# Graph attention on one core: for half the heads, the exponentials of two blocks are added by GpSimd and multiplied with 1e-8 once

## The chip, the cores and the metric

The kernel runs on one core of one Trainium2 chip. The metric is the time of one execution in device microseconds; the figure for a kernel is the median of several runs.

## The reference

Sixteen graphs (b) of 1024 nodes with 128 features go through two layers. Cut to what matters:

```python
# layer 0: attention with 8 heads of 16 features, over the edges of adj
h = relu(layernorm(x))
q, k, v = heads(h @ Wq.T + bq), heads(h @ Wk.T + bk), heads(h @ Wv.T + bv)
scores = where(adj == 0, -inf, einsum('bhnd,bhmd->bhnm', q, k) / sqrt(16))
attn = softmax(scores, axis=-1) * adj
attn = attn / (attn.sum(axis=-1, keepdims=True) + 1e-08)
x = x + merge(einsum('bhnm,bhmd->bhnd', attn, v)) @ Wo.T + bo
# layer 1: edges are "dilated" (row by row, every second neighbour of a long row is
# removed, which changes the rows after it), then three graph convolutions with batch norm
x = x + sage(relu(layernorm(x)), dilate(adj), ...)
```

With e = exp(score), masked, and w = e * adj, the attention of one node n is sum over m of w * v, divided by sum of w + 1e-8 * sum of e. The change is about the last term, 1e-8 times the sum of e.

## The kernel before

The program has two stages. In the first, attention of layer 0 runs together with the dilation of the edges (which needs only adj); in the second, the three graph convolutions run. Attention is TensorE, ScalarE and VectorE work; dilation is mostly VectorE work. A function takes a step of the one (`attention`), then steps of the other (`dilation`) up to a budget, so that both share the engines. The order of the instructions on TensorE (PE), ScalarE (ACT) and VectorE (DVE) is the order in which the program writes them; each engine works its queue in order. GpSimd (POOL) and the load queue on SyncE (SP) are in order too.

Attention goes over 16 graphs b, two halves c of the nodes n (512 each), eight blocks m of 128 neighbours, and two groups g of four heads: 512 half-steps. One half-step (b, c, m, g) does this:

- `scores` (L521 on): PE writes the mask and the scores of four heads into two PSUM tiles q = 0, 1 of 128x1024 (`sc`, L536 and L542). When a count of dilation comes first, the scores of the next half-step are drawn ahead of it (`made["next"]`).
- `values` (L466 on) of the half-step before: PE multiplies w with v, which has a column of ones for the sum of w (L469), and then e with `eps8`, a matrix that is 1e-8 in that same column (L474). Both add to one PSUM tile `acc[g]` from m = 0 to m = 7. This is the eps product of the text: four matmuls, which are eight in the trace.
- ACT makes e out of the scores, two tiles of 128x1024 (L579; ring of four tiles "e").
- DVE makes w = e * aT, two tiles (L584; ring of four tiles "w"), where aT is the transposed block of adj.

For g = 0 the block of adj that will be needed two steps later is transposed (`turn_over`, L487 on; `load` has brought it three steps ahead into a ring of three tiles "a"), and its mask is copied to other partitions by SP's queue (L498, L499).

Beside this, `conclude` divides the finished `acc` of the last half graph: `rd` is the reciprocal of the denominator (L395), and GpSimd copies it into `rden` (L399). At the end `judge` (L945 on) tests on DVE, over all of `rden`, that the denominators were in a sane range (L952, L953); if a test fails, a slow version of everything runs. `layer_norm_relu` uses GpSimd once for each norm, for a power of 8 numbers per partition (L272), whose result DVE takes up a half-step later (L274).

Of the kernel before, what the change touches and what calls it, by code (L numbers as in the profile page):

```python
# [10 lines left out]
F32 = mybir.dt.float32  # L11
BF = mybir.dt.bfloat16
# [4 lines left out]
ALU = mybir.AluOpType  # L17
AX = mybir.AxisListType
# [3 lines left out]
P = 128  # L22
# [2 lines left out]
NORM_EPS = 1e-12  # L25
BIG = 1e30
ROUNDS = 7


def tri(k):  # L30
# [4 lines left out]
def swept(ctx: ExitStack, tc: tile.TileContext, t: dict, out: bass.AP, flag: bass.AP):  # L35
# [8 lines left out]
    nc = tc.nc  # L44
    x, adj, nodemask = t["x"], t["adj"], t["nodemask"]
    B, N, D = x.shape
    H = 8
    HD = D // H
    NB = N // P
    HB = NB // 2  # L50
    HN = N // 2
# [112 lines left out]
    def first_part(p1):  # L164
# [15 lines left out]
        def load(i, queue=nc.sync):  # L180
            if i >= len(turns):
                return
            b, c, m = turns[i]
            a = pool.tile([P, HB, P], F32, name=f"a_{b}_{c}_{m}", tag="a", bufs=3)
            queue.dma_start(
                a, adj[b, c * HN : (c + 1) * HN, m * P : (m + 1) * P].rearrange("(k p) m -> p k m", p=P)
            )
            tiles[i] = a
# [36 lines left out]
            yield  # L225

        def node_masks():
            nr_f = pool.tile([B * NB, P], F32, name="nr_f", tag="w", bufs=4)
            nc.vector.tensor_copy(nr_f, nr_i)
            mps = ps_d.tile([P, 512], F32, name="mps", tag="d")  # L230
            nc.tensor.transpose(mps[:, : B * NB], nr_f, ident[: B * NB, : B * NB])
            nc.vector.tensor_copy(mf, mps[:, : B * NB])
            nc.vector.tensor_tensor(mf2, mf, mf, ALU.mult)
            nc.vector.tensor_scalar(
                kill.rearrange("p b k -> p (b k)"), mf, 0.0, -1e5, ALU.is_equal, ALU.mult
            )
# [16 lines left out]
        nc.vector.memset(eps8, 0.0)  # L253
        nc.vector.memset(eps8[:, HD : HD + 1], 1e-8)

        rden = one.tile([P, B * 2, HB, H], BF, name="rden")

        def layer_norm_relu(dst, src, name, lo=0, hi=NB):

# [117 lines left out]
        def conclude(b, c, acc, xt):  # L377

            yield False
            cx = small.tile([P, HB, H, HD], F32, name=f"cx_{b}_{c}", tag="cx", bufs=1)  # L380
            oTs = []
            for g in range(2):
                oT = small.tile([P, HN], F32, name=f"oT_{b}_{c}_{g}", tag="oT", bufs=2)
                nc.scalar.copy(oT, acc[g])
                oTs.append(oT)
            for g in range(2):
                yield True
                on = ps_m.tile([P, HB, 4, 32], F32, name=f"on_{b}_{c}_{g}", tag="m")
                for i in range(HB):
                    nc.tensor.transpose(  # L390
                        on[:, i, :, :].rearrange("p h d -> p (h d)"), oTs[g][:, i * P : (i + 1) * P], ident
                    )
                yield "evict by VectorE"
                rd = small.tile([P, HB, 4], F32, name=f"rd_{b}_{c}_{g}", tag="rd", bufs=2)
                nc.vector.reciprocal(rd.unsqueeze(3), on[:, :, :, HD : HD + 1])  # L395
                nc.vector.tensor_tensor(
                    cx[:, :, g::2, :], on[:, :, :, :HD], rd.unsqueeze(3).to_broadcast([P, HB, 4, HD]), ALU.mult
                )
                nc.gpsimd.tensor_copy(rden[:, 2 * b + c, :, 4 * g : 4 * g + 4], rd)  # L399
            yield True  # L400
            pc = ps_m.tile([P, 512], F32, name=f"pc_{b}_{c}", tag="m")
            for i in range(HB):
                nc.tensor.transpose(
                    pc[:, i * P : (i + 1) * P], cx[:, i, :, :].rearrange("p h d -> p (h d)"), ident
                )
            yield "evict"
            cxT = small.tile([P, HN], F32, name=f"cxT_{b}_{c}", tag="oT", bufs=2)
            nc.scalar.copy(cxT, pc)
            yield True
            pr = ps_m.tile([P, HB, D], F32, name=f"pr_{b}_{c}", tag="m")  # L410
            start_with(pr, bias3[:, 1, :])
            for i in range(HB):
                nc.tensor.matmul(
                    pr[:, i, :], cxT[:, i * P : (i + 1) * P], wts["Wo"], start=False, stop=(i == HB - 1)
                )
            yield "evict by VectorE"
            part = xt[:, c * HB : (c + 1) * HB, :]
            nc.vector.tensor_tensor(part, part, pr, ALU.add)
            if c == 1:
                yield False  # L420
                nc.sync.dma_start(x1_d[b], xt)
                yield from layer_norm_relu(xt, xt, f"b{b}")
                nc.sync.dma_start(h0_d[b], xt)
# [38 lines left out]
        def attention():  # L462

            late = None

            def values(acc, v1, m, g, es, ws):  # L466

                for j in range(4):
                    nc.tensor.matmul(  # L469
                        acc[g][32 * j : 32 * j + 32, :], v1[:, m, 2 * j + g, :],  # L470
                        ws[j // 2][:, j % 2, :], start=(m == 0), stop=False,
                    )
                for j in range(4):
                    nc.tensor.matmul(  # L474
                        acc[g][32 * j : 32 * j + 32, :], eps8,
                        es[j // 2][:, j % 2, :], start=False, stop=(m == NB - 1),
                    )

            def turn_over(i):
# [69 lines left out]
            for i, (b, c, m) in enumerate(turns):  # L549
                if m == 0:  # L550
                    if c == 0:
                        xt, _, _, v1 = ready[b]
                    acc = [ps_o.tile([P, HN], F32, name=f"acc_{b}_{c}_{g}", tag=f"acc{g}") for g in range(2)]
                    if c == 0 and b + 1 < B:
                        take_on(prepare(b + 1), len(beside))
                    if c == 1 and b + 1 == B:
                        take_on(begin_sage(), len(beside))
                if c == 1 and m == HB + 1:
                    load_x(b + 2)
                load(i + 3)  # L560
                aT = tiles[i][0]
                for g in range(2):
                    scs = scores(i, g)
                    go_on_with(f"half {c}")
                    if g == 0:
                        go_on_with("first")
                        turning = turn_over(i + 2)
                        next(turning, None)
                    else:
                        go_on_with(True)  # L570
                    if late:
                        values(*late)
                    elif g == 0:
                        node_masks()
                        go_on_with(True)
                    es, ws = [], []
                    for q in range(2):
                        e = pool.tile([P, 2, HN], F32, name=f"e_{b}_{c}_{m}_{g}_{q}", tag="e", bufs=4)
                        nc.scalar.activation(e, scs[q], AF.Exp, scale=1.0 / math.sqrt(HD))  # L579
                        es.append(e)  # L580
                    go_on_with("evict by VectorE")
                    for q in range(2):
                        w = pool.tile([P, 2, HN], F32, name=f"w_{b}_{c}_{m}_{g}_{q}", tag="w", bufs=4)
                        nc.vector.tensor_tensor(w, es[q], aT.to_broadcast([P, 2, HN]), ALU.mult)  # L584
                        ws.append(w)
                    late = (acc, v1, m, g, es, ws)
                    if m == 0 and g == 0 and i > 0:

                        take_on(conclude(*done), 1 if c == 0 else 0)
                        go_on_with(False)  # L590
                    go_on_with("evict")
                    if g == 0:
                        next(turning, None)
                    go_on_with(False)
                    if i + g + 1 < len(turns):
                        made["next"] = partial(scores, i + g, 1 - g)
                    yield
                tiles.pop(i)
                done = (b, c, acc, xt)
# [345 lines left out]
        def judge():  # L945
# [1 line left out]

            still = small.tile([P, 3], F32, name="still", bufs=1)
            nc.vector.tensor_reduce(still[:, 0:1], changed, AX.X, ALU.add)
            rd = rden.rearrange("p a i h -> p (a i h)")  # L950
            fits = pool.tile([P, B * NB * H], F32, name="fits", tag="kT")
            nc.vector.tensor_scalar(fits, rd, 1e25, None, ALU.is_le)  # L952
            nc.vector.scalar_tensor_tensor(  # L953
                fits, rd, 1e-30, fits, ALU.is_ge, ALU.mult, accum_out=still[:, 1:2]
            )
            nc.vector.tensor_scalar(still[:, 1:2], still[:, 1:2], -1.0, float(B * NB * H), ALU.mult, ALU.add)
            nc.vector.tensor_tensor(still[:, 0:1], still[:, 0:1], still[:, 1:2], ALU.add)
            nc.vector.tensor_reduce(still[:, 1:2], signs, AX.XYZ, ALU.add)
# [224 lines left out]
    with tc.manual_schedule(  # L1183
# [6 lines left out]
        for L in range(3):  # L1190
# [8 lines left out]
            for b in range(B):  # L1199
# [4 lines left out]
                for c in range(2):  # L1204
                    i = (L * B + b) * 2 + c
# [689 lines left out]
```

## Time and profile before

| what | us |
| --- | --- |
| median of 3 runs | 3561.78 (3560.0 to 3562.39) |
| the profiled execution, its own time | 3556.3 |
| span of the profiled execution | 3554.4 |
| busy in the span: PE / DVE / ACT / POOL | 3445.8 / 3174.0 / 2290.9 / 179.0 |

The profile is one execution. A group line gives line of code, engine, operation, tile written <- tiles read, the shape and the count; then busy us in all, the mean ns of one, and the time that the engine stood idle before such instructions with what ended it. A line in order of time gives start, length, engine, line, operation. A view by stage gives for each stretch the busy us of each engine. L numbers are lines of the kernel before. A wait is put down to the event that came last.

### The profile page before, as it was taken

The page shows a single profiled execution, that of the slowest core. Times are in us where ns is not written, and L with a number is a line of the kernel's source. Part 1 is how long each engine was busy: PE and PEld are TensorE (multiplying, and loading weights), DVE is VectorE, ACT ScalarE, POOL GpSimd, SP SyncE. Part 2 cuts the span into 40 slices and gives each one's busy share as a digit, 9 for nine tenths or more (in the row PEclk, how much of TensorE's full clock was granted, in tenths as well). Part 3 has the DMA queues.
Part 4 walks back from the last instruction along what each step waited for, and adds up shares of the span by engine and source line. Part 5 has one row for each costly group of instructions (what it writes and reads, how often), then busy time and mean ns, then how long its engine had stood idle before and what let it go on. Part 6 is the DMA issues. An engine that isn't in the chain of part 4 may idle for free.

```text
span 3554.4 us, 86070 instructions
## 1 busy us (share of the span) xinstructions
PE 3445.8 (97%) x34855; PEld 1893.8 (53%) x34855; DVE 3174.0 (89%) x5254; ACT 2290.9 (64%) x3781; POOL 179.0 (5%) x253
## 2 busy tenths in 40 slices
PE   8999999999999999999999999999999899999997
PEld 3333333333333333333333333338999899989996
DVE  7999999999989999999999999987878788878886
ACT  6699689679769869968976885873232333322224
POOL 2000000000000000000000000000000000000000
PEclk9999999999999999999999999999999999999999
DMA  7356356447537636735754763667999799989995
GB/s 231 102 169 201 123 159 199 142 135 214 168 111 222 195 116 201 227 111 170 235 157 133 235 205 110 209 213 285 331 331 326 266 328 328 329 295 333 333 332 184
DMA packets 650122, 772.27 MB, mean 217 GB/s; under 512 B 173264, under 2 KB 569168, under 8 KB 637424
## 3 DMA queue, kind: packets, MB, share of 16 engines
q1 hardware_dynamic: 632672, 708.58, 61.7%
q0 software_dynamic: 15456, 57.30, 4.9%
q8 instruction: 275, 4.51, 0.5%
q14 instruction: 135, 1.11, 0.1%
q10 hardware_dynamic: 1584, 0.79, 0.1%
HBM read 508.50 MB, written 157.29 MB: 187 GB/s over the span
## 4 chain that ended last, share of the span: by engine, by line
PE 48%; DVE 39%; ACT 6%; DMA 3%; issue 3%; SPq 1%; POOL 0%; ACTq 0%; DVEq 0%; POOLq 0%
DVE w L584 16%; PE pg L1108 16%; PE sc L542 6%; PE acc L469 5%; PE acc L474 5%; DVE wr L872 4%; PE pn L1079 2%; DVE hit L807 2%; ACT e L579 2%; PE sc L536 2%; PE own L1094 2%; PE py L1023 2%; DMA nomask<-nomask 1%; PE pt L1145 1%; DVE aT L142 1%
## 5 line engine op out<-in xcount | busy, mean ns | idle before, releaser
L584 DVE TENSOR_TENSOR w<-e,aT 128x1024 f32<-128x1024 f32 x1024 | 1204.2, 1217 | 91.2 <-ACT e L579 90.9
L579 ACT ACTIVATE e<-sc 128x1024 f32<-128x1024 f32 x1024 | 990.9, 1020 | 376.1 <-PE sc L542 375.0
L1108 PE MATMUL pg<-y,aT 128*128 128x128 f32 (+1 forms) x6144 | 738.0, 275 | 0.0
L1108 PEld LDWEIGHTS pg<-y,aT 128*128 128x128 f32 x6144 | 712.4, 192 | 0.0
L469 PE MATMUL acc<-w,v_both 128*32 128x512 f32 x4096 | 673.1, 607 | 8.6 <-DVE w L584 3.8
L474 PE MATMUL acc<-e,eps 128*32 128x512 f32 x4096 | 650.5, 596 | 0.0
L542 PE MATMUL sc<-qT,kT 32*128 32x512 f32 x4096 | 584.8, 641 | 0.0
L142 DVE SCALAR_TENSOR_TENSOR aT<-mr,aT 128x1024 f32<-128x1024 bf16 x384 | 458.9, 1217 | 0.0
L474 PEld LDWEIGHTS acc<-e,eps 128*32 128x32 f32 x4096 | 165.9, 110 | 295.1 <-issue 285.2
L1131 ACT ACTIVATE sq<-o 128x512 f32<-128x512 f32 x96 | 60.5, 631 | 363.4 <-DVE o L1126 363.4
L872 DVE TENSOR_TENSOR_SCAN wr<-rk 128x1024 f16<-128x1024 bf16 x128 | 291.7, 2279 | 0.0
L536 PEld LDWEIGHTS <-never 32*32 32x32 bf16 x8192 | 79.1, 88 | 345.3 <-issue 323.6
L536 PE MATMUL sc<-nomask,never 32*32 32x512 bf16 x8192 | 249.6, 385 | 12.5 <-ACT e L579 8.0
L469 PEld LDWEIGHTS acc<-w,v_both 128*32 128x32 f32 x4096 | 106.4, 108 | 233.9 <-DVE w L584 140.2
L542 PEld LDWEIGHTS sc<-qT,kT 32*128 32x128 f32 x4096 | 160.1, 183 | 116.6 <-issue 116.6
L487 PEld LDWEIGHTS pa<-ident,a 128*128 128x128 f32 x1024 | 108.2, 142 | 182.4 <-issue 143.5
L1146 ACT COPY hT<-pt 128x512 f32<-128x512 f32 x96 | 56.3, 587 | 224.2 <-PE pt L1145 223.2
L1126 DVE SCALAR_TENSOR_TENSOR o<-pg,rdeg,mine 128x128 f32<-128x128 f32 x384 | 108.1, 344 | 92.2 <-PE pg L1108 90.4
L885 ACT ACTIVATE wr<-wr,th 128x1024 f16<-128x1024 f16 x128 | 148.0, 1156 | 46.7 <-DVE wr L872 45.8
L487 PE MATMUL pa<-ident,a 128*128 128x128 f32 x1024 | 168.7, 288 | 7.0 <-DMA a<-in_adj 6.3
L494 ACT ACTIVATE nomask<-aT 128x512 bf16<-128x512 f32 x256 | 161.4, 630 | 8.1
L490 ACT COPY aT<-pa 128x512 f32<-128x512 f32 x256 | 151.6, 592 | 11.5 <-PE pa L487 6.8
(222 smaller groups left out, 3949.8 us busy)
## 6 DMA issues: line engine op xcount, KB each, us to landing
aT<-aT_d SPq DMA_DIRECT2D x94, 2048.0 KB, 9.0
mr<-mr_d SPq DMA_DIRECT2D x188, 512.0 KB, 5.8
aT_d<-aT SPq DMA_DIRECT2D x256, 256.0 KB, 4.0
a<-in_adj SPq DMA_DIRECT2D x253, 256.0 KB, 4.0
ad<-in_adj SPq DMA_DIRECT2D x112, 512.0 KB, 4.1
nomask<-nomask SPq DMA_DIRECT2D x512, 96.0 KB, 2.7
nomask<-nomask SPq DMA_DIRECT2D x512, 64.0 KB, 2.6
nomask<-nomask SPq DMA_DIRECT2D x512, 32.0 KB, 2.6
```

What stands on the lines that cost most here:

```text
L142: nc.vector.scalar_tensor_tensor(part, mrs[h][:, j : j + 2, :].rearrange("p j n -> p (j n)"), 0.0, part, ALU.is_equal, ALU.mult)
L469: nc.tensor.matmul(acc[g][32 * j : 32 * j + 32, :], v1[:, m, 2 * j + g, :], ws[j // 2][:, j % 2, :], start=(m == 0), stop=False,)
L474: nc.tensor.matmul(acc[g][32 * j : 32 * j + 32, :], eps8, es[j // 2][:, j % 2, :], start=False, stop=(m == NB - 1),)
L487: nc.tensor.transpose(pa[:, k * P : (k + 1) * P], a[:, k, :], ident)
L490: nc.scalar.copy(aT[:, 0, :], pa)
L494: nc.scalar.activation(nomask[:, 0, :], aT[:, 0, :], AF.Relu, bias=1.0, scale=-1e38, accum_out=zeros[:, i : i + 1])
L536: nc.tensor.matmul(scs[j // 2][to : to + 32, j % 2, :], never[rows, rows], nomask[rows, j, :], start=True, stop=False, tile_position=(32 * ...
L542: nc.tensor.matmul(scs[j // 2][:, j % 2, :], kT[rows, mm], qTs[c][rows, g, :], start=False, stop=True, tile_position=(32 * j, 0),)
L579: nc.scalar.activation(e, scs[q], AF.Exp, scale=1.0 / math.sqrt(HD))
L584: nc.vector.tensor_tensor(w, es[q], aT.to_broadcast([P, 2, HN]), ALU.mult)
L872: nc.vector.tensor_tensor_scan(wrs[b], rk(b, 1, N + 1), rk(b, 2, N + 2), -1023.0, ALU.add, ALU.add)
L1108: nc.tensor.matmul(pg[:, i // 2, at : at + width], aT[:, j, i * P : (i + 1) * P], y[:, j, :width], start=(j == 0), stop=(j == NB - 1),)
```

## The change

For the heads of g = 0 and the blocks m = 0 to 5, the e of an even block is kept (two tiles "kept"); GpSimd adds the e of the odd block to it, and the eps product is made once for both blocks, at the head of the next even half-step of g = 0. For g = 1 and for m = 6 and 7 nothing changes. To have room for the kept tiles, the ring w has three tiles for four, the ring a two for three (the third first tile borrows one that dilation uses later), and `rden` goes: GpSimd tests `rd` at once, in four small instructions, and adds up the results, which `judge` sums.

```diff
+PAIRED = 6
...
-            a = pool.tile([P, HB, P], F32, name=f"a_{b}_{c}_{m}", tag="a", bufs=3)
+            where, tag = (shared, "ad") if i == 2 else (pool, "a")
+            a = where.tile([P, HB, P], F32, name=f"a_{b}_{c}_{m}", tag=tag, bufs=2)
...
-        rden = one.tile([P, B * 2, HB, H], BF, name="rden")
+        rfits = one.tile([P, HB, 4], F32, name="rfits")
+        nc.gpsimd.memset(rfits, 0.0)
...
-                nc.gpsimd.tensor_copy(rden[:, 2 * b + c, :, 4 * g : 4 * g + 4], rd)
+                fit = small.tile([P, 2, HB, 4], F32, name=f"fit_{b}_{c}_{g}", tag="fit", bufs=1)
+                nc.gpsimd.tensor_scalar(fit[:, 0], rd, 1e25, None, ALU.is_le)
+                nc.gpsimd.tensor_scalar(fit[:, 1], rd, 1e-30, None, ALU.is_ge)
+                nc.gpsimd.tensor_tensor(fit[:, 0], fit[:, 0], fit[:, 1], ALU.mult)
+                nc.gpsimd.tensor_tensor(rfits, rfits, fit[:, 0], ALU.add)
...
             def values(acc, v1, m, g, es, ws):
 
                 for j in range(4):
                     nc.tensor.matmul(
                         acc[g][32 * j : 32 * j + 32, :], v1[:, m, 2 * j + g, :],
                         ws[j // 2][:, j % 2, :], start=(m == 0), stop=False,
                     )
+                if g == 1 or m >= PAIRED:
+                    exponentials(acc, g, es, m == NB - 1)
+
+            def exponentials(acc, g, es, stop):
                 for j in range(4):
                     nc.tensor.matmul(
                         acc[g][32 * j : 32 * j + 32, :], eps8,
-                        es[j // 2][:, j % 2, :], start=False, stop=(m == NB - 1),
+                        es[j // 2][:, j % 2, :], start=False, stop=stop,
                     )
...
                 for g in range(2):
+                    if both and g == 0 and m % 2 == 0:
+                        exponentials(*both, False)
+                        both = None
                     scs = scores(i, g)
...
-                        e = pool.tile([P, 2, HN], F32, name=f"e_{b}_{c}_{m}_{g}_{q}", tag="e", bufs=4)
+                        kept = g == 0 and m < PAIRED and m % 2 == 0
+                        e = pool.tile(
+                            [P, 2, HN], F32, name=f"e_{b}_{c}_{m}_{g}_{q}",
+                            tag="kept" if kept else "e", bufs=2 if kept else 4,
+                        )
...
-                        w = pool.tile([P, 2, HN], F32, name=f"w_{b}_{c}_{m}_{g}_{q}", tag="w", bufs=4)
+                        w = pool.tile([P, 2, HN], F32, name=f"w_{b}_{c}_{m}_{g}_{q}", tag="w", bufs=3)
...
                     late = (acc, v1, m, g, es, ws)
+                    if g == 0 and m < PAIRED and m % 2 == 0:
+                        first = es
+                    elif g == 0 and m < PAIRED:
+                        for to, e in zip(first, es):
+                            nc.gpsimd.tensor_tensor(to, to, e, ALU.add)
+                        both = (acc, g, first)
...
-            rd = rden.rearrange("p a i h -> p (a i h)")
-            fits = pool.tile([P, B * NB * H], F32, name="fits", tag="kT")
-            nc.vector.tensor_scalar(fits, rd, 1e25, None, ALU.is_le)
-            nc.vector.scalar_tensor_tensor(
-                fits, rd, 1e-30, fits, ALU.is_ge, ALU.mult, accum_out=still[:, 1:2]
-            )
+            nc.vector.tensor_reduce(still[:, 1:2], rfits, AX.XY, ALU.add)
```

More of the change, by code (lines that the diff above doesn't have):

```diff
@@ L227, in node_masks @@
         def node_masks():
-            nr_f = pool.tile([B * NB, P], F32, name="nr_f", tag="w", bufs=4)
+            nr_f = pool.tile([B * NB, P], F32, name="nr_f", tag="w", bufs=3)
             nc.vector.tensor_copy(nr_f, nr_i)
@@ L464, in attention @@
             late = None
+            first = both = None
             def values(acc, v1, m, g, es, ws):
```

## The prediction

> **What bounds the kernel now.** I read the busy shares first, then the same by stage, then the groups of the attention stage, then single places in order of time.
>
> ```profile
> 0.00:2412.00 2412.00, 2362.34 (x25784) 860.84 (x25784) 2264.10 (x3414) 1917.83 (x3003) 135.75 (x173) 1.00 0.58 173
> 2412.00:3554.40 1142.40, 1083.49 (x9071) 1032.99 (x9071) 909.90 (x1842) 373.03 (x779) 43.23 (x80) 0.98 0.87 311
> ```
>
> These two rows are the stages (window, length, busy of PE, PEld, DVE, ACT, POOL, then the granted clock, DMA share, GB/s). The change lies in the first, up to the last products of attention at 2412 us. There VectorE (DVE) is busy for 2264.1 of 2412 us, so 147.9 us are all the idle time it has. TensorE (PE) reads 98%, but a matmul that waits for an operand counts as busy there, so its true load is lower. GpSimd (POOL) is nearly free: 135.75 us. The clock is at full speed, so it is no term of the sum. The second stage (1142.4 us) is left as it is.
>
> ```profile
> L584 DVE TENSOR_TENSOR w<-e,aT 128x1024 f32<-128x1024 f32 x1024 | 1204.2, 1217 | 91.2 <-ACT e L579 90.9
> L474 PE MATMUL acc<-e,eps 128*32 128x512 f32 x4096 | 650.5, 596 | 0.0
> L716 POOL MEMSET go_on<- 128x2048 bf16 x8 | 14.4, 1805 | 136.5 <-DVE hit L807 80.8 <-PE sc L542 53.0 <-DVE rk L664 2.7
> L717 POOL MEMSET go_on<- 128x16 bf16 x8 | 1.4, 171 | 0.5
> ```
>
> The groups (busy us, mean ns of one, idle before): the products w are half of DVE's work, and both operands of w lie in SBUF. L474 is the eps product that the change makes less often: 512 calls, 650.5/512 = 1.27 us each (a call in an unbroken run takes 1.04). In the chain of waits of this stage w has 23.7% and L474 6.6%: both engines alternate on the path, DVE with the larger part.
>
> Now the rows that decide, all in order of time, for the only GpSimd instruction of before that reads two operands from SBUF, the small power of L272 (8 elements):
>
> ```profile
> 1126.98 2.28 DVE L872 TENSOR_TENSOR_SCAN wr<-rk 128x1024 f16<-128x1024 bf16 x1
> 1127.22 3.48 POOL L272 TENSOR_TENSOR rs_b<-rs_b,minus_half 128x8 f32<-128x8 f32 x1 [37.54 <-DVE rs_b L271]
> 1129.18 2.33 DVE L584 TENSOR_TENSOR w<-e,aT 128x1024 f32<-128x1024 f32 x2
> 1372.81 0.54 DVE L889 TENSOR_SCALAR er<-wr,th 128x1024 bf16<-128x1024 f16 x1
> 1373.05 1.80 POOL L272 TENSOR_TENSOR rs_a<-rs_a,minus_half 128x8 f32<-128x8 f32 x1 [74.17 <-ACT rk L673]
> ```
>
> The same instruction takes 3.48 us when it comes 0.24 us after the start of a DVE instruction with two SBUF operands, and 1.80 where DVE is in a short one (1.64 where it reduces one tensor, at 1225.29 us). All 13 that met a long two-operand instruction 0.23 to 0.27 us after its start took 3.45 to 3.54 us, 1.8 more than 1.64, which is about what was left of it. So a GpSimd read and a two-operand DVE instruction exclude each other. The products behind it (2.33 for two, as elsewhere) show no delay, but 8 elements are read in no time. The reverse case, DVE held up by a long GpSimd read, no row shows.
>
> **What goes.** 32 halves of a batch times 3 pairs = 96 eps calls. PE is relieved of 96 x 1.04 to 1.27 = 100 to 122 us. GpSimd loses 64 casts (64 x 0.198 = 12.7 us), which nobody waits for. The closing test loses two 128x1024 passes on DVE (0.7 + 1.2 us, once).
>
> **What comes: 192 adds of 128x1024 f32 on GpSimd.** Their price isn't in the trace. The nearest rows are the two memsets: (1805 - 171)/(2048 - 16) = 0.80 ns an element for one stream. Two streams read, with the write beside them, make 0.17 + 2 x 0.82 = 1.82 us; three streams one after the other 2.64. I take 2.0, nearer to the lower end, because the slope already has a write in it. 192 x 2.0 = 384 us of GpSimd, which had 2276 us free.
>
> What the adds do to DVE: bounds 0 (only the reader on GpSimd gives way) and the full time of each add. Of DVE's time in this stage some 85% (sum of the groups with two SBUF operands) can collide, and right behind the exponentials more: at the 96 places the first w begins 0.87 us (median) after its exponential ends, and both w follow each other. I put the two adds into the 96 places by the instructions' own times: an add begins when its exponential is done and the two-operand instruction then running has ended, and a two-operand instruction that comes during an add waits for its end. Per place DVE is 3.7 us late (3.3 with adds of 1.8, 4.9 with 2.6): 96 x 3.7 = 354 us. I take this full exclusion, since the rows above show exclusion and not sharing, and the time on the shared way has to be spent by one or the other. From it comes off what DVE's idle time takes up. PE is relieved, so DVE waits less for scores; half of 147.9 = 74 us. Sum: 354 - 74 = +280 us.
>
> [...]
>
> **Waits that are added.** PE: the joint eps call stands in PE's queue right behind the products of w of the odd block, and scores, the next values and the dilation's small matmuls stand behind it. At the 96 places the eps call starts 4.69 us (median; 3.84 at the fifth percentile) after the first exponential ends; two adds end 2 x 2.0 + 0.06 = 4.1 after it if nothing holds them up, so it seldom waits. If they are held up by DVE, the w before it are late too. 0 taken; without that cover 1 to 2 us x 96.
>
> GpSimd's queue: the power for the norm ahead of attention (15 times in this stage after the first) comes at m = 1, 3.4 to 5.5 us after the first exponential, or early in m = 2, so it can stand behind the adds by up to 2 us. Its reader L274 on DVE starts 2.7 to 5.4 us after it, and it needs 1.64 to 1.8. 0 taken, at most 30. The one for the second norm comes at m = 7, where no add is. The first loads of dilation on this queue can be late by two adds, once.
>
> Kept exponentials (two tiles): ScalarE's next kept one needs the joint eps call to be through, which stands ahead of its scores on PE. Only where scores are drawn ahead of a count (56 counts, 3 of 16 half-steps: some 10) is it new: at most 10 x 3 us. 0 taken.
>
> **Edits with one answer.** Three w tiles for four: the second w of a half-step now needs the first four value matmuls of the half-step before. In the trace it starts 0.96 us (fifth percentile) to 4.2 us after them, never before. Two a tiles for three: the load of block i+3 needs the transposes of i+1; on SP's queue stand ahead of it the mask copies of i+1, which already wait for them. The four tests of rd: 256 small instructions of about 0.2 us on GpSimd, nobody behind; at most 256 x 0.1 us of DVE.
>
> **The rivals.** Ends faster: DVE isn't held up by the adds. Then PE's relief counts. By the chain 6.6% of 2412 x 96/512 = 30 us; if PE set the pace everywhere, 100. About -50: 3512 us. For it: the w behind the power of L272 keep 2.33. Against it: the 3.48 us rows. It decides if w in the paired half-steps stays at 1.22 us. Ends slower in another way: DVE always goes first, the adds live on its gaps (0.15 of 4.6 us, plus 0.3 idle, in a half-step) until PE stands at the joint eps call and DVE runs dry; then some 3 us of each pair are lost: 96 x 3 = 290, or 3850 us, with adds of 8 us and PE waiting for POOL.
>
> **How the numbers follow.** The profiled execution took 3556.3 us (span 3554.4 and 1.9 around it); the median of the runs is 3561.8, 5.5 more. Forecast: 3556.3 + 280 + 5.5 = 3842. Chances: DVE held up 0.78, adds starved 0.07, no hold 0.15, of which 0.02 falls within 0.2% of no change (about what a measurement can tell): faster 0.13, same 0.02, slower 0.85. The first case alone runs from adds of 1.82 us, 0.85 of them met and all idle time used (192 x 1.82 x 0.85 - 148 = +149: 3711) to 2.64 us with nothing taken up and the small bills added (192 x 2.64 x 0.94 + 60 = +536: 4098). The range 3600 to 4000 leaves out the faster case and a few hundredths at the top, and has room for a partial hold below 3711.
>
> **What would show it.** Right: POOL some 350 us busier or more, DVE's busy time in the stage up by 250 to 400 us although it has the same work, with long w (2 us and over) in the half-steps of odd m and g = 0; L474 at 3328 matmuls; the second stage as long as before. Wrong: w at 1217 ns throughout and the first stage shorter (the first rival), or DVE's idle time up with PE waiting for the add (the second).

## The result, and the profile after

The changed kernel takes 3937.5 us (median of 4 runs, 3933.2 to 3942.9), the kernel before 3560.9 (4 runs): a ratio of 1.106, interval 1.104 to 1.108. The profiled execution took 3933.2 us, 376.9 more than that of before.

The view by stage, in the columns of before (window, length, busy of PE, PEld, DVE, ACT, POOL, clock, DMA share, GB/s):

```profile
0.00:2791.00 2791.00, 2477.68 (x25016) 854.83 (x25016) 2661.12 (x3413) 1923.67 (x3003) 884.84 (x552) 0.96 0.50 149
2791.00:3931.40 1140.40, 1081.29 (x9071) 1030.87 (x9071) 907.98 (x1840) 372.86 (x779) 47.59 (x86) 0.98 0.87 312
```

The second stage is as long as before (1140.4 for 1142.4 us). The first went from 2412 to 2791 us, +379. VectorE has the same work there (3413 instructions for 3414) and is busy for 397.0 us longer; its idle time fell from 147.9 to 2791.0 - 2661.1 = 129.9, by 18. 397 - 18 = 379: the whole loss stands in VectorE's busy time.

The groups (busy us, mean ns of one | idle before, and what ended it):

```profile
L606 DVE TENSOR_TENSOR w<-e,aT 128x1024 f32<-128x1024 f32 x1024 | 1405.9, 1413 | 81.0 <-ACT e L601 77.9
L613 POOL TENSOR_TENSOR e<-e,e 128x1024 f32<-128x1024 f32 x192 | 563.6, 2955 | 1011.7 <-ACT e L601 625.3
L900 DVE TENSOR_TENSOR_SCAN wr<-rk 128x1024 f16<-128x1024 bf16 x128 | 320.5, 2504 | 0.0
L489 PE MATMUL acc<-e,eps 128*32 128x512 f32 x3328 | 645.3, 629 | 31.7 <-POOL e L613 31.7
```

The products w cost 201.7 us more, though nothing about them was changed: 95 of the 1024 take longer, in the median 3.37 us, the others 1.22 as before. The rest of the 397 us is in the other instructions of VectorE, the scan for one. In all, 188 VectorE instructions (beside 192 adds) take over 0.3 us longer than their like before, 397 us together. L489 has 3328 matmuls, as the change says.

One place in order of time (start, length, engine, line, operation), with a pair of adds:

```profile
311.56 4.52 DVE L606 TENSOR_TENSOR w<-e,aT 128x1024 f32<-128x1024 f32 x2 [0.73 <-ACT e L601]
316.00 4.44 DVE L900 TENSOR_TENSOR_SCAN wr<-rk 128x1024 f16<-128x1024 bf16 x1
...
311.60 6.69 POOL L613 TENSOR_TENSOR e<-e,e 128x1024 f32<-128x1024 f32 x2 [10.03 <-ACT e L601]
```

The two engines take turns. The first w (1.22 us) runs and the first add waits for it; then the add runs and the second w waits for 2.15 us (4.52 for two in place of 2.36); then w runs and the second add waits; then the scan waits for 2.16 us (4.44 in place of 2.28). An add takes 2.34 to 2.40 us where it meets nothing and 3.3 to 3.4 behind a w; its record holds the wait, and so does VectorE's. That is why VectorE looks busy and not idle.

### The profile page after: what moved, and what is told of

Same layout as the page of the kernel before. It is cut to its first block, busy times and chain, and to the rows that moved or that the text cites. A ratio compares the mean times of both kernels' runs of the same rounds, so it can differ in the third digit from the quotient of the medians.

```text
span 3931.4 us, 85633 instructions
## 1 busy us (share of the span) xinstructions
PE 3559.0 (91%) x34087; PEld 1885.7 (48%) x34087; DVE 3569.1 (91%) x5252; ACT 2296.5 (58%) x3781; POOL 932.4 (24%) x638
## 4 chain that ended last, share of the span: by engine, by line
DVE 45%; PE 36%; issue 9%; ACT 6%; DMA 2%; POOL 1%; SPq 1%; ACTq 0%; DVEq 0%; POOLq 0%
DVE w L606 22%; PE pg L1131 14%; DVE wr L900 4%; PE acc L480 4%; PE sc L557 4%; PE acc L489 3%; ACT e L601 2%; PE pn L1102 2%; PE own L1117 2%; DVE rk L714 2%; DVE er L920 2%; DVE hit L835 2%; PE py L1046 2%; PE pt L1168 1%; DVE er L929 1%
## 5 line engine op out<-in xcount | busy, mean ns | idle before, releaser
L606 DVE TENSOR_TENSOR w<-e,aT 128x1024 f32<-128x1024 f32 x1024 | 1405.9, 1413 | 81.0 <-ACT e L601 77.9
L480 PE MATMUL acc<-w,v_both 128*32 128x512 f32 x4096 | 786.9, 630 | 162.6 <-DVE w L606 153.9
L613 POOL TENSOR_TENSOR e<-e,e 128x1024 f32<-128x1024 f32 x192 | 563.6, 2955 | 1011.7 <-ACT e L601 625.3
L489 PE MATMUL acc<-e,eps 128*32 128x512 f32 x3328 | 645.3, 629 | 31.7 <-POOL e L613 31.7
L557 PE MATMUL sc<-qT,kT 32*128 32x512 f32 x4096 | 596.9, 653 | 0.0
L480 PEld LDWEIGHTS acc<-w,v_both 128*32 128x32 f32 x4096 | 116.1, 110 | 474.1 <-DVE w L606 392.2
L900 DVE TENSOR_TENSOR_SCAN wr<-rk 128x1024 f16<-128x1024 bf16 x128 | 320.5, 2504 | 0.0
L551 PE MATMUL sc<-nomask,never 32*32 32x512 bf16 x8192 | 263.3, 394 | 26.3 <-ACT e L601 21.8
L489 PEld LDWEIGHTS acc<-e,eps 128*32 128x32 f32 x3328 | 141.5, 114 | 299.8 <-issue 235.2
```

Source lines behind the costliest of these rows:

```text
L480: nc.tensor.matmul(acc[g][32 * j : 32 * j + 32, :], v1[:, m, 2 * j + g, :], ws[j // 2][:, j % 2, :], start=(m == 0), stop=False,)
L489: nc.tensor.matmul(acc[g][32 * j : 32 * j + 32, :], eps8, es[j // 2][:, j % 2, :], start=False, stop=stop,)
L551: nc.tensor.matmul(scs[j // 2][to : to + 32, j % 2, :], never[rows, rows], nomask[rows, j, :], start=True, stop=False, tile_position=(32 * ...
L557: nc.tensor.matmul(scs[j // 2][:, j % 2, :], kT[rows, mm], qTs[c][rows, g, :], start=False, stop=True, tile_position=(32 * j, 0),)
L613: nc.gpsimd.tensor_tensor(to, to, e, ALU.add)
L900: nc.vector.tensor_tensor_scan(wrs[b], rk(b, 1, N + 1), rk(b, 2, N + 2), -1023.0, ALU.add, ALU.add)
```

## The experiments

The theory, from the rows above (a w of 3.37 us in place of 1.22, an add of 3.3 to 3.4 in place of 2.34 to 2.40): a GpSimd instruction that reads SBUF and a VectorE instruction with two SBUF operands exclude each other, so each add costs VectorE, which sets the pace of the stage (busy for 2661.1 of 2791.0 us), some 2.1 us (397/192). The rivals: the smaller rings and the tests cost the time; or PE does, standing at the joint product until the add is there. The kernel before beside these runs took 3557 to 3559 us. The L numbers of each profile are lines of that run's kernel.

**The rest of the change alone.**

```diff
-PAIRED = 6
+PAIRED = 0
```

> The changed kernel with no pair at all: every eps product is made by itself again and GpSimd adds nothing; the smaller rings (w, a), the borrowed tile and the four small tests of rd on GpSimd stay. Theory (the adds hold up VectorE, the rest costs nothing): 3555 to 3585 us, VectorE's busy time within 25 us of before. Rival (the rings or the tests cost the time): a large part of the 376 us stays, 3650 us or more.

3549.1 us, ratio 0.9969 (0.9957 to 0.9982): slightly faster than before.

```profile
L606 DVE TENSOR_TENSOR w<-e,aT 128x1024 f32<-128x1024 f32 x1024 | 1204.6, 1217 | 89.8 <-ACT e L601 89.1
L489 PE MATMUL acc<-e,eps 128*32 128x512 f32 x4096 | 655.1, 594 | 0.0
```

VectorE is busy for 3172.9 us in the whole span, where it was 3174.0 before. The rings and the tests are not the cause; the adds and the joint products hold all of the loss, 388 us. What makes this kernel some 10 us faster wasn't taken apart: 1.9 us are the two passes that leave the closing test.

**The adds without a use.**

```diff
-                if g == 1 or m >= PAIRED:
+                if True:
                     exponentials(acc, g, es, m == NB - 1)
...
-                        for to, e in zip(first, es):
+                        for to, e in zip(spare, es):
                             nc.gpsimd.tensor_tensor(to, to, e, ALU.add)
```

> All eps products as before, one for each block; GpSimd still does the 192 adds of 128x1024 at the same places, into two tiles of its own that nobody reads (the result is not used). So PE waits for no add and does all its former work. Theory (each add holds up VectorE for its length, about 2.1 us): 192 x 2.1 = 400 us more, 3900 to 3990 us, one long w of about 3.4 us at nearly each paired half-step. Rival (the time is lost because PE stands at the joint product until the add is there): 3560 to 3600 us.

3939.8 us, ratio 1.107 (1.105 to 1.109), as slow as the changed kernel, though PE waits for no add here and makes every product.

```profile
L604 DVE TENSOR_TENSOR w<-e,aT 128x1024 f32<-128x1024 f32 x1024 | 1409.1, 1417 | 91.5 <-ACT e L599 89.6
L609 POOL TENSOR_TENSOR spare<-spare,e 128x1024 f32<-128x1024 f32 x192 | 568.6, 2981 | 1019.4 <-ACT e L599 1019.3
L491 PE MATMUL acc<-e,eps 128*32 128x512 f32 x4096 | 757.4, 624 | 0.0
```

The same long w, the same adds. The adds by themselves are enough for the loss; PE's wait at the joint product (31.7 us of idle above) costs nothing that can be seen.

**GpSimd writes and doesn't read.**

```diff
-                            nc.gpsimd.tensor_tensor(to, to, e, ALU.add)
+                            nc.gpsimd.tensor_copy(to[:, 0, 0:1], e[:, 0, 0:1])
+                            filled = to.rearrange("p a n -> p (a n)").bitcast(BF)
+                            nc.gpsimd.memset(filled, 0.0)
+                            nc.gpsimd.memset(filled[:, 0:HN], 0.0)
```

> As with the unused adds, but in place of each add GpSimd reads one number per partition of e, and then only writes: two memsets, by the rows of before 1.80 + 0.58 = 2.4 us, as long as an add. Theory (reads of GpSimd and two-operand instructions of VectorE exclude each other): no hold for w, 3560 to 3620 us. Rival (any long work on GpSimd holds VectorE up): 3850 us or more.

3577.1 us, ratio 1.005 (1.003 to 1.007): 28 us above the kernel without pairs, of which the last section says more.

```profile
L604 DVE TENSOR_TENSOR w<-e,aT 128x1024 f32<-128x1024 f32 x1024 | 1204.8, 1217 | 94.8 <-ACT e L599 93.7
L611 POOL MEMSET spare<- 128x2048 bf16 x192 | 346.0, 1802 | 5.6
```

GpSimd was as long in the same places (1.80 + 0.52 us, 192 times) and not one w is longer (none takes over 1.24 us). It is the reading that holds w up, not that GpSimd works.

**GpSimd reads one stream.**

```diff
-                            nc.gpsimd.tensor_tensor(to, to, e, ALU.add)
+                            nc.gpsimd.tensor_copy(to, e)
```

> As with the unused adds, but GpSimd copies e (one stream read and one written, 128x1024) in place of the add. Theory (the hold is as long as GpSimd reads): one stream takes about 1.0 us by the memset's slope, so 192 x 1.0 = 190 us more than without: 3700 to 3790 us. Rival (a fixed hold for each instruction, whatever it reads): 3900 us or more.

3683.7 us, ratio 1.035 (1.034 to 1.037): 135 us above the kernel without pairs, less than expected.

```profile
L604 DVE TENSOR_TENSOR w<-e,aT 128x1024 f32<-128x1024 f32 x1024 | 1275.0, 1286 | 85.9 <-ACT e L599 84.6 <-PE acc L482 0.9
L609 POOL COPY spare<-e 128x1024 f32<-128x1024 f32 x192 | 307.7, 1630 | 1013.7 <-ACT e L599 1013.7
```

The copy takes 1.04 us where it meets nothing, and 84 of the w are 0.84 us longer in the median. So the hold is not a fixed sum for each instruction: it is 0.84 us of a copy's 1.04 and 2.15 of an add's 2.35, in both some 0.2 us less than the GpSimd instruction takes alone. Whether the number of streams or the length of the reading sets it wasn't taken apart. The expectation took the copy's whole length for the hold and every one as met.

**A third of the pairs.**

```diff
-PAIRED = 6
+PAIRED = 2
```

> The change with one pair for each half graph (blocks 0 and 1) in place of three: 64 adds, 32 eps calls less. Theory (each add costs its hold, nothing is taken up): a third of the 388 us between the changed kernel and the one without pairs, 3549 + 130 = 3665 to 3690 us. Rival (idle time takes up the first adds, and only more of them cost): below 3630 us.

3675.5 us, ratio 1.033 (1.031 to 1.035): 126 us above the kernel without pairs, where a third of 388 is 129. The loss goes with the number of adds, and the first ones aren't taken up by idle time.

**No adds, the products as changed** (the odd blocks' share of 1e-8 times the sum is left out).

```diff
-                        for to, e in zip(first, es):
-                            nc.gpsimd.tensor_tensor(to, to, e, ALU.add)
```

> The changed kernel without the 192 adds; the joint eps product is made of the even block alone (the odd block's share of 1e-8 times the sum is left out). What is left is PE's relief of 96 eps calls. Theory: 30 to 100 us faster than before, 3460 to 3530 us. Rival (VectorE alone sets the pace, PE's relief is worth nothing): 3550 to 3570 us. Rival (rings, kept tiles or the later place of the product cost time): above 3600 us.

3547.4 us, ratio 0.9965 (0.9954 to 0.9976): 2 us from the kernel without pairs, less than its own runs differ (3539 to 3552).

```profile
L489 PE MATMUL acc<-e,eps 128*32 128x512 f32 x3328 | 548.6, 596 | 0.0
```

PE was relieved of 106 us of eps products (548.6 us busy in L489 for 655.1) and no gain can be seen. This fell between what was expected, close to the rival that PE's relief is worth nothing: the theory had 30 to 100 us for it.

**The adds on VectorE.**

```diff
-                            nc.gpsimd.tensor_tensor(to, to, e, ALU.add)
+                            nc.vector.tensor_tensor(to, to, e, ALU.add)
```

> The changed kernel with the 192 adds on VectorE itself, at the same places of the program; all else as changed. Theory (an add on GpSimd costs VectorE the add's length of some 2.1 us, because the two exclude each other): VectorE does one in 1.13 us (the spacing of two w), so 192 x 1.13 = 217 us more than without adds (3547): 3750 to 3780 us, 160 to 190 us faster than with GpSimd. Rival (the time comes from the adds being late for PE): about as slow as with GpSimd, 3900 us or more.

3730.3 us, ratio 1.049 (1.047 to 1.050).

```profile
L613 DVE TENSOR_TENSOR e<-e,e 128x1024 f32<-128x1024 f32 x192 | 225.9, 1218 | 0.0
```

VectorE does the 192 adds itself in 226 us, and the kernel is 207 us faster than with the adds on the nearly idle GpSimd; the hold that GpSimd put on VectorE was longer than the work. It came out 20 us under the range: VectorE's idle time in the stage fell to 107 us, from 137 without adds, so here some of the added work did go into idle time.

**A greater relief for PE.** All 512 eps products read e as bf16, with one matmul in the trace where f32 has two (2048 for 4096, 395 ns for 596):

```diff
-        eps8 = one.tile([P, 32], F32, name="eps8")
+        eps8 = one.tile([P, 32], BF, name="eps8")
...
-                        es[j // 2][:, j % 2, :], start=False, stop=(m == NB - 1),
+                        es[j // 2][:, j % 2, :].bitcast(BF)[:, 1::2], start=False, stop=(m == NB - 1),
```

> The kernel before with one edit: all 512 eps products read the upper 16 bits of e as bf16 (the eps matrix in bf16 too), so that one pass is made for each and not the passes of f32; PE is relieved by some 0.7 us a call, 350 us in all, more than three times as much as in the change. Theory as it stands after the first runs (VectorE alone sets the pace of the stage, PE's relief is worth nothing): 3530 to 3560 us. Rival (PE and VectorE share the path, a large relief counts): 3420 to 3500 us.

3527.2 us, ratio 0.9915 (0.9898 to 0.9932), 30 us faster than before and 3 us under the theory's range.

```profile
L474 PE MATMUL acc<-e,eps 128*32 128x512 bf16 x2048 | 311.5, 395 | 0.0
L584 DVE TENSOR_TENSOR w<-e,aT 128x1024 f32<-128x1024 f32 x1024 | 1203.9, 1217 | 62.0 <-ACT e L579 61.6
```

PE was relieved of 650.5 - 311.5 = 339 us and 30 came of it, a tenth. "Nothing" was too strong: the scores come earlier (ScalarE waits 310.3 us for them where it waited 375.0), and VectorE waits 62.0 us for exponentials before w where it waited 91.2.

**Both gains together** (the kernel without pairs, with the bf16 products):

> The changed kernel without pairs (smaller rings, tests of rd on GpSimd), with all 512 eps products made from the upper 16 bits of e as bf16. Theory: the two gains are in different places (VectorE's idle time in the stage; the end of the stage and the closing test) and add up: 3557 - 30 - 10 = 3510 to 3522 us. Rival (both use up the same idle time): no better than the bf16 products alone, 3524 to 3530 us.

3518.9 us, ratio 0.9897 (0.9880 to 0.9914): in the theory's range, faster than the kernel before by 1%, and than the changed one by 419 us. Its four runs spread from 3511.9 to 3527.6 us, so that the two gains add up in full is likely and not certain. It keeps the aim of the change (less time on the 1e-8 term) and gives GpSimd no adds.

## Why the prediction held, and where its sum was off

It said 3842 us in a range of 3600 to 4000, slower with 0.85; 3937 lies in the range and on that side. By its own steps:

- **Bound.** Right: VectorE sets the pace of the stage. The row of the power that took 3.48 us behind a scan was the right one to read; it showed exclusion in one direction, and the other direction is what cost the time.
- **The hold.** Full exclusion was right (2.15 us of an add's 2.35), the size too small: 354 us, measured 397, or 397/192 = 2.07 us for an add. The price of an add was taken as 2.0 from the memset's slope; it is 2.34 to 2.40, of which VectorE sees 2.15. And nearly every add met an instruction that had to wait (188 held for 192 adds): 2.07 of 2.15 us, 0.96, where the places gave 0.92.
- **What idle time takes up.** The step that was off most: 74 us were to come off, measured 18. Two things could have filled idle time, and neither did by much. PE's relief was to make VectorE wait less; without adds it is worth 2 us. And delays could have fallen into gaps; a third of the pairs cost a third of the time, so the first ones don't. Why the delays leave so much of the idle time as it was stays open. The two errors, 43 and 56 us, add up to the 99 us between +280 and the measured +379 of the stage.
- **The waits taken at nothing.** Right for the rings, the a tiles and the tests: the kernel without pairs isn't slower. The tests were mis-sized all the same: one takes 0.27 to 1.24 us on GpSimd, not 0.2, 201 us in all and not 51, which nobody waited for. PE waited 31.7 us for adds and ScalarE 39.2, which cost nothing that can be seen, as the kernel with unused adds is as slow. The clock, no term of the sum, fell to 0.96 in the stage; the last section says why no time is put down to it.
- **The rivals.** "Not held up" was excluded by the long w, and would have been mis-priced: -50 us, where the run without adds is 2 us below the kernel without pairs and 11 below the kernel before. "Adds starved" was excluded too: an add waits for one instruction and then has its turn; the longest of the 192 takes 4.40 us.

## What to carry to other kernels

The idle GpSimd wasn't free here beside a busy VectorE: look first at how many SBUF operands the VectorE instructions have. For w, which has two (1.22 us, 3.37 when held), the adds on GpSimd, which read SBUF, were time taken from VectorE: 2.1 us for each add of 128x1024 that VectorE does itself in 1.2. Price such work so, or measure it. Busy time that grew with an unchanged instruction count was here a wait inside the records. And before work is moved off an engine, take it away altogether in one run: here that would have shown that the relief was worth 2 us of 3549, less than the runs differ.

## What the runs showed of the hardware

Small one-operand instructions of VectorE were held up as well. In the changed kernel, in order of time:

```profile
1420.21 4.72 POOL L613 TENSOR_TENSOR e<-e,e 128x1024 f32<-128x1024 f32 x2 [0.27 <-ACT e L601]
...
1420.42 2.24 DVE L781 TENSOR_SCALAR cs<-cs 128x16 f32<-128x16 f32 x1
```

A tensor-scalar of 16 f32 numbers, 0.17 us elsewhere, takes 2.24 during an add. It is the kind of instruction that the memsets held up too, in the run where GpSimd only writes:

```profile
L822 DVE TENSOR_SCALAR v<-v 128x16 f32<-128x16 f32 x56 | 22.3, 398 | 1.6
L823 DVE TENSOR_SCALAR v<-v 128x16 f32<-128x16 f32 x56 | 20.9, 373 | 0.0
```

Of each 56, 9 were 0.4 to 1.6 us late and end as a memset does, so the means went from 0.17 or 0.18 us to 0.40 and 0.37. The two wait at the same time: together they cover 25.9 us, for 14.3 in the kernel without pairs. That is 12 of the 28 us that this kernel lost against it (VectorE is busy for 3189.1 us in all, for 3172.9); what the rest is wasn't taken apart. Not held up by the adds were the norm statistics (12 within adds, 0.28 us at most), reductions (1.20), and instructions with an operand in PSUM (`v<-parts,gone`, 0.17). What sets these apart from the tensor-scalars no run shows.

The granted clock fell with the waits: 0.96 in the first stage of the changed kernel for 1.00 before. It goes along with the loss in the unused adds too (0.965 over the span, for 0.991), and of the value matmuls 95% take up to 0.97 us, where before it was 0.62. But a loss of this kind doesn't need it: in the run with copies the clock was 0.988 over the span, and VectorE was busy for 3315.3 us, for 3172.9 without pairs, 142 us beside a loss of 135. As VectorE's busy time explains the whole difference in the changed kernel as well, no share is put down to the clock; no run held it apart.
